# Fourteen units of unmasked rows moved into the triangle's stage, with a joined matmul and a triangle that goes by way of DRAM

## The chip, the cores and the metric

The kernel runs on one core of one Trainium2 chip. The core has a matmul engine (PE, with its weight loads PEld shown apart), a vector engine (DVE), a scalar engine (ACT), a GpSimd engine (POOL) and a sync engine (SP) that only issues transfers. Each engine works through its own list of instructions in order and waits on semaphores. On chip there is SBUF, which engines and transfers use, and PSUM, eight banks of 2 KB in each of 128 partitions, into which PE writes. The metric is the device time in microseconds; the time before is the median of three runs.

## The reference

The input x has the shape (1, 512, 512, 64), in float32. Two layers are applied, each after a group norm over the whole image:

```python
x = x + L0(_gn(x))
x = x + L1(_gn(x))

# L0, with m the 0/1 mask over the 512 positions, D = H = 64
xn = _ln(x, norm_w, norm_b)
left = (xn @ left_w + left_b) * mask          # mask[i, j] = m[i] * m[j]
right = (xn @ right_w + right_b) * mask
left = left * sigmoid(xn @ lgate_w + lgate_b)
right = right * sigmoid(xn @ rgate_w + rgate_b)
out_gate = sigmoid(xn @ ogate_w + ogate_b)
out = einsum('bkjd,bkid->bijd', left, right)   # the "triangle"
out = _ln(out, onorm_w, onorm_b) @ out_w + out_b
return out * out_gate

# L1: the lowest 12 x 12 modes of a 2-D Fourier transform, mixed over
# the channels by complex weights, and transformed back
```

Where a row or a column of the image is masked, the triangle is zero there, so that the output before the gate is a constant row, the transformed bias. The gate is still computed everywhere.

## The kernel before

The kernel sorts the 512 positions by the mask at run time. If at most K = 256 of them are unmasked, which is the case with these inputs, `compact` runs (line 621). Sorted rows 0 to 255 form "half 0", which holds all masked-in rows; rows 256 to 511 form "half 1", which holds only rows whose triangle is zero (these are the change's "unmasked rows", in the sense that no mask or triangle is applied to them).

`compact` has these stages, one after the other:

- **Statistics and compaction** (lines 653 to 700): all of x is read, and the 256 x 256 positions that matter are kept.
- **Projection** (703 to 809): left and right are computed and stored channel by channel to `left_d` and `right_d` in DRAM.
- **Triangle** (848 to 879): for each of 64 channels, left and right are loaded (line 855), each turned by four PE transposes into a PSUM tile (859), copied to SBUF by DVE (864) or ACT (867, two halves), and multiplied in four matmuls (873). DVE applies the masks and writes the result into `tri`, which is the large SBUF array `places`, at a stride of 128 elements (877). No other work runs in this stage.
- **Products and gates** (886 to 1258): one loop over steps `s`, written out by hand, in which each engine's order is the order of the code. Eight steps make a unit. A step handles 8 groups of 64 channels for each of 128 partitions. The first 8 units (`first`) are **products**: the triangle's layer norm and `out_w`, of which the result goes to `u_d` in DRAM. Then follow 32 **gate units** `(jc, half)`, alternating half 1 and half 0 for each of 16 blocks of 32 columns `jc`.
- **Tail** (1260 to 1400): the modes of the second layer, and its output.

In the loop PE works ahead: at step `s` it transposes the data of step `s + LEAD` (`LEAD` = 13, `transpose`, 986), and multiplies by the centring matrix for `s + LEAD - 1` (`centered`, 1005); then it multiplies by the gate's matrix for `s` itself (`times` with `gate_x`, 1002). For products, `centered` instead forms eight matmuls over 64 rows each with `both`, a matrix that holds the centring and `out_w` side by side (1013), and ACT takes the two parts out of PSUM in two instructions (1030, 1031). For gates, ACT takes the transposed data (997) and squares the centred ones (1027). DVE sums the squares over channels (1035), makes the row statistics of the new x (1120), scales by the inverse deviation (1218) and adds the gate's bias (1224). ACT applies the sigmoid (1169). POOL multiplies by the triangle's output, or by the constant row for half 1 (`gated`, 1061), and adds x (`added`, 1065). In products POOL adds a bias (1222).

On the queues: POOL gathers x, 1 MB at a time (637). SP stores the new x (1081), loads the triangle's output of one block by `load_u` (1049), whose 32 transfers each have an address held in a register, loaded first (645), and stores the partial modes of a block (`save`, 1098, four transfers per block); `fetch` and `columns` turn these into sums of modes every 8 units. `load_u` for the next block is issued at each half-1 unit (1242), so once in two units, into one of two buffers, places 5 and 6. x has five buffers (`RING`).

PSUM before: in the products two tiles of two banks each for `y_ps`; in the gates two banks each for `c_ps` and `w_ps`; in both two banks for transposes, one for `scratch` (sums, factors, biases) and one for the modes.

Of the kernel before, what the change touches and what calls it, by code (L numbers as in the profile page):

```python
# [17 lines left out]
P = 128  # L18
N = 512
# [27 lines left out]
def conv_preact_kernel(ctx: ExitStack, tc: tile.TileContext, t: dict):  # L47
# [573 lines left out]
    def compact(fc):  # L621
# [4 lines left out]
        modes_d = dram.tile([N, M2, C], F32, name="modes_d")  # L626
# [203 lines left out]
        with tc.tile_pool(name="tri", bufs=1) as trp:  # L830

            places = trp.tile([P, K * 2 * C], F32, name="places")
            tri = places.rearrange("p (j r c) -> p j r c", r=2, c=C)
# [14 lines left out]
            with tc.tile_pool(name="ti", bufs=4) as ip, tc.tile_pool(name="tt", bufs=3) as tp, tc.tile_pool(  # L848
                name="tpt", bufs=4, space=PSUM
            ) as ps_t, tc.tile_pool(name="tpo", bufs=3, space=PSUM) as ps_o:  # L850
                for c in range(C):
                    sides = []
                    for name, src in (("left", left_d), ("right", right_d)):
                        raw = ip.tile([P, 2, K], F32, name=name + "_raw")
                        nc.sync.dma_start(raw, src[c].rearrange("(b p) k -> p b k", p=P))
                        tps = ps_t.tile([P, 2, K], F32, name="side_ps")
                        for kb in range(2):
                            for b in range(2):
                                nc.tensor.transpose(
                                    tps[:, kb, b * P : (b + 1) * P], raw[:, b, kb * P : (kb + 1) * P], ident  # L860
                                )
                        side = tp.tile([P, 2, K], F32, name=name + "_t")
                        if name == "left":
                            nc.vector.tensor_copy(side, tps)
                        else:
                            for kb in range(2):
                                nc.scalar.mul(side[:, kb, :], tps[:, kb, :], mask_k2[:, kb : kb + 1])
                        sides.append(side)
                    lt, rt = sides
                    ps = ps_o.tile([P, 2, K], F32, name="tri_c_ps")  # L870
                    for r in range(2):
                        for kb in range(2):
                            nc.tensor.matmul(
                                ps[:, r, :], rt[:, kb, r * P : (r + 1) * P], lt[:, kb, :], start=(kb == 0), stop=(kb == 1)
                            )
                    for r in range(2):
                        nc.vector.scalar_tensor_tensor(  # L877
                            tri[:, :, r, c], ps[:, r, :], slot_t[:, r, 1:2], mask_s, ALU.mult, ALU.mult
                        )

# [3 lines left out]
            first = K * 2 // 64  # L884

            units = [(jc, half) for jc in range(NJ) for half in ((1, 0) if jc < NJ - 1 else (0, 1))]
            total_g = (first + len(units)) * SIZE
            with tc.manual_schedule(), tc.tile_pool(name="late", bufs=1) as lp:
# [23 lines left out]
                def columns(h, pool):  # L912

                    q = P if h < 3 else P - JC
                    by = modes_t.rearrange("p (m k) c -> p m (k c)", k=2)
                    ps = pool.tile([P, 4, P], F32, name="t_ps").rearrange("p i k -> p (i k)")[:, : MODES * M2]
                    ps = ps.rearrange("p (m n) -> p m n", m=MODES)
                    for m in range(MODES):
                        nc.tensor.matmul(ps[:, m, :], by[:q, m, :], col_basis[:q, h, :], start=h < 3 or m == 0, stop=h < 3)
                    if h < 3:  # L920
                        nc.vector.tensor_add(sums, sums, ps)
                    return ps

                def fetch(h):

                    q = P if h < 3 else P - JC
                    (nc.scalar if h == 3 else nc.sync).dma_start(modes_t[:q], modes_d[h * P : h * P + q])
# [26 lines left out]
                with tc.tile_pool(name="np_x", bufs=LEAD + 2) as tp, tc.tile_pool(  # L954
# [7 lines left out]
                    ps_y = products.enter_context(tc.tile_pool(name="np_b", bufs=2, space=PSUM))  # L962
# [3 lines left out]
                    for h in range(2):  # L966
                        hs = slice(h * C, (h + 1) * C)
                        nc.vector.tensor_copy(both[hs, :C], center[hs, hs])
                        nc.vector.tensor_copy(both[hs, C:], weights["out"][hs, hs])
# [12 lines left out]

                    def x_of(k):
                        return place(order[k % RING])

                    def transpose(s):
                        k, n = divmod(s, SIZE)
                        flat = (place(k) if k < first else x_of(k - first)).rearrange("p n c -> p (n c)")
# [5 lines left out]
                        if k < first:  # L994
                            nc.scalar.copy(xts[s], tps)
                        else:
                            nc.scalar.activation(xts[s], tps, AF.Identity, bias=ab1[:, 2:3])  # L997
# [7 lines left out]
                    def centered(s):  # L1005
                        if s >= first * SIZE:
                            return times(ps_c, "c_ps", s, center_x)

                        ps = ps_y.tile([P, 2, 4, P], F32, name="y_ps")
                        for i in range(4):  # L1010
                            for h in range(2):
                                hs = slice(h * C, (h + 1) * C)
                                nc.tensor.matmul(ps[:, h, i, :], xts[s][hs, i, :], both[hs], start=True, stop=True)  # L1013

                        xts[s] = tp.tile([P, 4, P], F32, name="xt_c")
                        return ps

                    def raw(s):
                        return xts[s].rearrange("p i (h c) -> p (i h) c", h=2)

                    def squared(s, cps):
# [4 lines left out]
                        if s >= first * SIZE:  # L1026
                            nc.scalar.activation(sq, cps, AF.Square)  # L1027
                        else:
# [14 lines left out]
                    def load(k, r):  # L1043
                        jc, half = units[k]
# [41 lines left out]
                    def transform(k, r):  # L1086
                        jc, half = units[k]
                        if k % 2 == 0 and r == 0:
                            fs[jc] = ps_f.tile([P, N], F32, name="f_ps")
                        for g in range(4):  # L1090
                            o = r * JC + 8 * g
                            nc.tensor.matmul(
                                fs[jc][32 * g : 32 * g + 32, :], hb[:, 2 * half + r, :],
                                x_of(k)[:, o : o + 8, :].rearrange("p j c -> p (j c)"),
                                start=(k % 2 == 0 and r == 0), stop=(k % 2 == 1 and r == 1), tile_position=(0, 32 * g),
                            )

                    def save(jc):
                        ft = places[:, 7 * 64 * C + M2 * C : 7 * 64 * C + 32 * C].rearrange("p (j c) -> p j c", c=C)
                        nc.scalar.copy(ft.rearrange("p j c -> p (j c)"), fs.pop(jc))  # L1100
# [10 lines left out]
                        for g in range(4):  # L1111
                            o = jc * JC + 8 * g
                            queue = nc.scalar if jc == NJ - 2 else nc.sync
                            queue.dma_start(modes_d[o : o + 8].rearrange("j m c -> m j c"), ft[32 * g : 32 * g + M2])

                    def statistics(k, groups):
                        if k % 4 == 0 and 0 in groups:
                            st[k // 4] = s1.tile([P, G, 4, 6], F32, name="stats2c", bufs=2)
                        for g in groups:
                            nc.vector.bn_stats(st[k // 4][:, g, k % 4, :], x_of(k)[:, :, 2 * g : 2 * g + 2])  # L1120
# [22 lines left out]

                    for s in range(-LEAD, total_g + 2 * SIZE):
                        k, n = divmod(s, SIZE)
                        v = k - first

                        def held(i):
                            return 0 <= v - i < len(units)

                        if s + LEAD < total_g:
                            transpose(s + LEAD)
                        wps = cps = None
                        if s + LEAD - 1 == first * SIZE:
# [3 lines left out]
                        if 0 <= s < total_g:  # L1158
                            wps = raw(s) if k < first else times(ps_w, "w_ps", s, gate_x)
                            del xts[s]  # L1160
                        if 0 <= s + LEAD - 1 < total_g:
                            cps = centered(s + LEAD - 1)
                        if n in (0, 4) and held(1):
                            transform(v - 1, n // 4)

                        if n % 2 == 0:
                            i, c = (0, n // 2 - 1) if n >= 2 else (1, 3)
                            if held(i):
                                nc.scalar.activation(zs[v - i, c], zs[v - i, c], AF.Sigmoid)  # L1169
                        if n == 5 and 0 <= k + 1 < first + len(units):  # L1170
# [3 lines left out]
                        if n == 5 and held(1) and v % 2 == 0:  # L1174
                            save(units[v - 1][0])
                        if n == 3 and held(2) and v % 4 == 1:
                            join_squares(v // 4 - 1)

                        if n % 2 == 1:
                            i, c = (0, (n - 3) // 2) if n >= 3 else (1, 3)  # L1180
                            if held(i) and (v - i, c) != (last, 3):
                                gated(v - i, c)
                            elif held(i):
                                finished()
                        else:
                            i, c = (0, (n - 4) // 2) if n >= 4 else (1, 2 + n // 2)
                            if held(i) and (v - i, c) != (last, 3):
                                added(v - i, c)
                        if 0 <= v + 3 < len(units):
                            if n == 3:  # L1190
                                load(v + 3, 0)
                            if n == 6:
                                load(v + 3, 1)
# [284 lines left out]
```

## Time and profile before

| what | value |
|---|---|
| median of 3 runs | 1802.41 us (1800.54 to 1804.09) |
| profiled execution: span, first to last instruction | 1803.7 us |
| PE, DVE, ACT, POOL busy | 90%, 79%, 53%, 52% of the span |
| triangle's stage | about 450 to 648 us |
| products (first to last of their matmuls `y_ps`) | 649.4 to 757 us |
| gates (first `w_ps` to the last bias add) | 775.7 to 1475 us |
| tail | 1475 to 1803.7 us |
| moved by DMA | 484.94 MB, mean 269 GB/s |

The profiled execution is known by its span, and it lies inside the range of the three timed runs, 1.3 us over their median; the page lists nothing outside the span. In a row of the groups of instructions the number after the count is the busy time, then the mean of one instruction in ns, then the engine's idle time just before, and what ended it.

### The profile page before, as it was taken

To read this page: it belongs to the slowest core of one execution; us is meant where nothing else is said; L and a number is where in the kernel's file an instruction comes from. 1 tells how busy PE (TensorE), PEld (TensorE's weight loads), DVE (VectorE), ACT (ScalarE), POOL (GpSimd) and SP (SyncE) were. 2 spreads that over 40 slices of the span, in tenths; PEclk is the share of its full clock that TensorE was granted. 3 is DMA by queue.
4 is the path that set the end of the run, shared out by engine and by line. 5 is a ranking of instruction groups with operands and counts; after the bars stand their busy time and mean duration, and the time that the engine had idled before them with its cause. 6 is when DMAs were issued, how large, how long until landed. Compare 5 with 4: busy or idle time off the path is not lost. (4 is left out here: it accounts for less than half of the span.)

```text
span 1803.7 us, 33076 instructions
## 1 busy us (share of the span) xinstructions
PE 1618.5 (90%) x11174; PEld 1259.6 (70%) x11174; DVE 1426.0 (79%) x2980; ACT 964.2 (53%) x1724; POOL 935.2 (52%) x695
## 2 busy tenths in 40 slices
PE   6879799997899999999999999999999976998772
PEld 6666666662787778887888888888888854665331
DVE  7889678887455547888999999999999995865452
ACT  3655566663222269976777777777777741011000
POOL 4656111111000006788999999999999892111110
PEclk9989899999899999999999999999999977555555
DMA  7999278878655504577777777687677699999999
GB/s 283 389 374 372 98 197 231 228 234 232 206 180 176 178 21 164 222 235 255 259 243 257 264 259 237 227 302 260 236 235 270 215 284 414 426 427 426 427 427 385
DMA packets 194642, 484.94 MB, mean 269 GB/s; under 512 B 35616, under 2 KB 135200, under 8 KB 153504
## 3 DMA queue, kind: packets, MB, share of 16 engines
q1 hardware_dynamic: 158160, 262.09, 41.7%
q0 software_dynamic: 32832, 218.45, 33.4%
q10 hardware_dynamic: 3472, 2.20, 0.5%
q8 instruction: 91, 1.49, 0.3%
q14 instruction: 87, 0.71, 0.1%
HBM read 294.83 MB, written 187.83 MB: 268 GB/s over the span
## 5 line engine op out<-in xcount | busy, mean ns | idle before, releaser
L1002 PE MATMUL w_ps<-gate_x,xt_c 128*128 128x128 f32 x2048 | 280.4, 281 | 29.2 <-DVE z_t L1218 23.8
L1065 POOL TENSOR_TENSOR places<-places,z_t 128x1024 f32<-128x1024 f32 x127 | 301.1, 2371 | 8.1
L1002 PEld LDWEIGHTS w_ps<-gate_x,xt_c 128*128 128x128 f32 x2048 | 252.2, 194 | 44.5 <-DVE z_t L1218 39.9
L1002 PE MATMUL c_ps<-center_x,xt_c 128*128 128x128 f32 x2048 | 276.8, 279 | 0.9 <-ACT xt_c L1031 0.6
L1002 PEld LDWEIGHTS c_ps<-center_x,xt_c 128*128 128x128 f32 x2048 | 252.8, 194 | 3.9 <-ACT xt_c L997 2.2
L1384 PE MATMUL l_ps<-places,rinv 24*128 24x512 f32 x512 | 206.3, 1108 | 29.4 <-DVE places L1391 19.3
L1120 DVE BATCH_NORM_STATS2 stats2c<-places 128x6 f32<-128x128 f32 x1024 | 220.5, 278 | 7.8 <-POOL places L1065 7.8
L1035 DVE TENSOR_REDUCE scratch<-sq_c 128x16 f32<-128x1024 f32 x160 | 194.5, 1216 | 27.9 <-ACT sq_c L1030 23.7
L1169 ACT ACTIVATE z_t<-z_t 128x1024 f32<-128x1024 f32 x128 | 135.5, 1058 | 129.0 <-DVE z_t L1224 113.7
L1222 POOL TENSOR_TENSOR z_t<-z_t,bias_row_out 128x1024 f32<-128x1024 f32 x32 | 75.7, 2365 | 246.5 <-PE y_ps L1013 222.5
L992 PE MATMUL t_ps<-c_ident,places 128*128 128x128 f32 x1280 | 199.5, 279 | 2.0 <-DVE places L877 1.3
L1384 PEld LDWEIGHTS l_ps<-places,rinv 24*128 24x128 f32 x512 | 119.0, 298 | 111.6 <-DVE places L1391 59.4
L992 PEld LDWEIGHTS t_ps<-c_ident,places 128*128 128x128 f32 x1280 | 144.9, 142 | 62.3 <-issue 53.7
L997 ACT ACTIVATE xt_c<-t_ps,ab_xc 128x512 f32<-128x512 f32 x256 | 176.2, 688 | 13.9 <-PE t_ps L992 12.9
L1218 DVE TENSOR_TENSOR z_t<-w_ps,rs_n 128x512 f32<-128x512 f32 x256 | 171.7, 671 | 7.8 <-PE w_ps L1002 7.8
L1027 ACT ACTIVATE sq_c<-c_ps 128x512 f32<-128x512 f32 x256 | 150.7, 589 | 31.6 <-PE c_ps L1002 31.2
L687 DVE BATCH_NORM_STATS2 stats1c<-x_ps 128x6 f32<-128x512 f32 x256 | 156.3, 681 | 13.8 <-PE x_ps L686 12.6
L1224 DVE TENSOR_TENSOR z_t<-z_t,scratch 128x1024 f32<-128x1024 f32 x128 | 156.3, 1221 | 10.3 <-ACT rs_n L1041 4.1
L1061 POOL TENSOR_TENSOR z_t<-z_t,places 128x1024 f32<-128x1024 f32 x64 | 151.8, 2371 | 13.9 <-ACT z_t L1169 13.8
L1391 DVE TENSOR_TENSOR places<-places,l_ps 128x512 f32<-128x512 f32 x176 | 110.4, 683 | 53.7 <-DMA places<-x_h,dst_i 44.4
L1061 POOL TENSOR_TENSOR z_t<-z_t,bias_row_out 128x1024 f32<-128x1024 f32 x63 | 149.3, 2370 | 5.6 <-ACT z_t L1169 4.4
L672 ACT COPY xc<-xg 128x128 f32 x352 | 105.0, 298 | 69.0 <-POOL xc L672 45.2
(213 smaller groups left out, 2619.0 us busy)
## 6 DMA issues: line engine op xcount, KB each, us to landing
x_h<-places SPq DMA_DIRECT2D x64, 1024.0 KB
out_x<-places SPq DMA_DIRECT2D x44, 1024.0 KB
places<-u_d SPq DMA_DIRECT2D x512, 64.0 KB
out_x<-lx_t SPq DMA_DIRECT2D x20, 1024.0 KB
rbc<-rs_d POOLq DMA_DIRECT2D x32, 512.0 KB
left_d<-o_c SPq DMA_DIRECT2D x64, 256.0 KB
right_d<-o_c SPq DMA_DIRECT2D x64, 256.0 KB
left_raw<-left_d SPq DMA_DIRECT2D x64, 256.0 KB
```

The costliest lines, as they stand in the source:

```text
L687: nc.vector.bn_stats(stats[:, 0, 16 * (jc % quarter) + 4 * r + c, :], ps.rearrange("p i k -> p (i k)"))
L992: nc.tensor.transpose(tps[:, i, :], flat[:, o : o + P], ident)
L997: nc.scalar.activation(xts[s], tps, AF.Identity, bias=ab1[:, 2:3])
L1002: nc.tensor.matmul(ps[:, 2 * i : 2 * i + 2, :], xts[s][:, i, :], w, start=True, stop=True)
L1027: nc.scalar.activation(sq, cps, AF.Square)
L1035: nc.vector.tensor_reduce(totals[k % 2][:, 8 * (n - 1) : 8 * (n + 1)], sqs.pop(s // 2), AX.X, ALU.add)
L1061: nc.gpsimd.tensor_mul(zs[k, c], zs[k, c], u)
L1065: nc.gpsimd.tensor_add(xr, xr, zs.pop((k, c)))
L1120: nc.vector.bn_stats(st[k // 4][:, g, k % 4, :], x_of(k)[:, :, 2 * g : 2 * g + 2])
L1218: nc.vector.tensor_mul(z[:, 8 * odd : 8 * odd + 8, :], wps, rs)
L1224: nc.vector.tensor_add(z, z, bias_ps["ogate"].unsqueeze(1).to_broadcast([P, 16, C]))
L1384: nc.tensor.matmul(ps.rearrange("p j o -> p (j o)"), rinv[h, b, :], it[h], start=True, stop=True, tile_position=(32 * g, 0),)
```

## The change

Fourteen of the 16 half-1 gate units, which need nothing of the triangle, are put ahead of the products, and the triangle's instructions are spread over their steps. The order of units becomes 14 early gate units, 8 product units (`None`), gate unit (14, 1), then (jc, 0) for jc = 0 to 15, then (15, 1): 40 units, as before.

- **Centre and gate as one matmul** for the early units: `both` first holds `center_x` and `gate_x`, so that `centered` makes both results in the form that the products used, and ACT copies the second part out of PSUM. `both` is refilled for the products.
- **The triangle** is issued in halves of a channel: `triangle(h)`, `turn_side`, `keep_side`, `masked`. `halves` gives two halves to each of the 12 steps -12 to -1, and spreads the other 104 over the steps 0 to 93. Loads run four sides ahead. The two matmul halves share one PSUM tile `tri_pair` (one bank), and `side_ps` and `y_ps` have one buffer each in that stretch, `y_ps` of two banks.
- **By way of DRAM**: `masked` writes to `staged`, and SP stores each channel to `tri_d`. The products load `tri_d` channel-major, two transfers of 256 KB for each two steps (`load_product`), in place of transposes. Their matmuls then take it directly.
- **`load_u`** is now needed for 16 units in a row and is issued once a unit, at its step 2.
- **Modes** are kept apart by half: `save` runs for each unit but one, and `fetch` and `columns` run eight times in place of four.

```diff
-        modes_d = dram.tile([N, M2, C], F32, name="modes_d")
+        modes_d = [dram.tile([N, M2, C], F32, name=f"modes_d{h}") for h in range(2)]
+        tri_d = dram.tile([C, K, K], F32, name="tri_d")
...
-                for c in range(C):
-                    sides = []
...
-            first = K * 2 // 64
-            units = [(jc, half) for jc in range(NJ) for half in ((1, 0) if jc < NJ - 1 else (0, 1))]
+            early = NJ - 2
+            first = early + K * 2 // 64
+            units = [(jc, 1) for jc in range(early)] + [None] * (first - early) + [(early, 1)]
+            units += [(jc, 0) for jc in range(NJ)] + [(NJ - 1, 1)]
...
+                    ps_y = products.enter_context(tc.tile_pool(name="np_a", bufs=1, space=PSUM))
+                    ps_s = products.enter_context(tc.tile_pool(name="np_i", bufs=1, space=PSUM))
+                    ps_o = products.enter_context(tc.tile_pool(name="np_o", bufs=1, space=PSUM))
+                    tri_pair = ps_o.tile([P, 2, K], F32, name="tri_c_ps")
...
+                    beside(center_x, gate_x)
...
+                    def load_product(q):
+                        for h in range(2):
+                            nc.sync.dma_start(
+                                products_t[q % 4][h * C : (h + 1) * C],
+                                tri_d.rearrange("c j i -> c (j i)")[:, (2 * q + h) * 2 * N : (2 * q + h + 1) * 2 * N],
+                            )
...
+                        if units[s // SIZE] is None:
+                            q, e = divmod(s - early * SIZE, 2)
+                            of = products_t[q % 4][:, e * N : (e + 1) * N].rearrange("p (i k) -> p i k", i=4)
+                        else:
+                            of = xts[s]
                         for i in range(4):
                             for h in range(2):
                                 hs = slice(h * C, (h + 1) * C)
-                                nc.tensor.matmul(ps[:, h, i, :], xts[s][hs, i, :], both[hs], start=True, stop=True)
+                                nc.tensor.matmul(ps[:, h, i, :], of[hs, i, :], both[hs], start=True, stop=True)
...
+                    def load_side(g):
+                        c, right = divmod(g, 2)
+                        nc.sync.dma_start(loose[g % 4], (left_d, right_d)[right][c].rearrange("(b p) k -> p b k", p=P))
+                    def turn_side(g):
+                        tps = side_of[g] = ps_s.tile([P, 2, K], F32, name="side_ps")
...
+                    def keep_side(g):
+                        tps, side = side_of.pop(g), turned_sides[g % 4]
+                        if g % 2:
+                            for kb in range(2):
+                                nc.scalar.mul(side[:, kb, :], tps[:, kb, :], mask_k2[:, kb : kb + 1])
+                        else:
+                            nc.vector.tensor_copy(side[:, 0], tps[:, 0])
+                            nc.scalar.copy(side[:, 1], tps[:, 1])
+                    def triangle(h):
+                        c, b = divmod(h, 2)
+                        lt, rt = (turned_sides[(2 * c + i) % 4] for i in range(2))
+                        tri_of[h] = tri_pair[:, b]
+                        for kb in range(2):
+                            nc.tensor.matmul(
+                                tri_of[h], lt[:, kb, b * P : (b + 1) * P], rt[:, kb, :], start=(kb == 0), stop=(kb == 1)
+                            )
+                    def masked(h):
+                        c, b = divmod(h, 2)
+                        nc.vector.scalar_tensor_tensor(
+                            staged[c % 4][:, b], tri_of.pop(h), slot_t[:, b, 1:2], mask_s, ALU.mult, ALU.mult
+                        )
+                        if b == 1:
+                            nc.sync.dma_start(tri_d[c].rearrange("(b p) i -> p b i", p=P), staged[c % 4])
...
+                    begin, even, until = 1 - LEAD, 0, early * SIZE - LEAD - 5
+                    for h in range(2 * C):
+                        at = begin + h // 2
+                        if at >= even:
+                            done = 2 * (even - begin)
+                            at = even + (h - done) * (until - even) // (2 * C - done)
+                        halves.setdefault(at, []).append(h)
...
                         if s + LEAD < total_g:
                             transpose(s + LEAD)
+                        for h in unmasked:
+                            masked(h)
...
                         if 0 <= s + LEAD - 1 < total_g:
                             cps = centered(s + LEAD - 1)
...
+                        for h in mine:
+                            triangle(h)
+                            turn_next(h + 2)
+                            if h != mine[-1]:
+                                keep_next(h + 2)
...
                         if cps is not None:
                             squared(s + LEAD - 1, cps)
+                        if mine:
+                            keep_next(mine[-1] + 2)
...
+                        for h in mine[:-1]:
+                            masked(h)
+                        unmasked = mine[-1:]
...
-                        if s == first * SIZE:
+                        if s == first * SIZE + 2:
                             load_u(0)
-                        if n == 4 and v % 2 == 0 and 0 <= v < len(units) - 2:
-                            load_u(v // 2 + 1)
+                        if n == 2 and first < k < last - 1:
+                            load_u(k - first)
```

`turn_next` calls `turn_side` and issues the load of the side four further on; `keep_next` calls `keep_side`. In the loop the order within a step is: transposes, the last step's `masked`, `centered`, the modes' matmuls, triangle and turn, ACT's sigmoid, root and `squared`, `keep_next`, then POOL's and DVE's gate work as before.

## The prediction

> **What bounds the kernel now.** First the busy time by stretch: the triangle, the products, the gates (DMA share and GB/s end each line).
>
> ```profile
> core 0: us, PE busy (x) PEld busy (x) DVE busy (x) ACT busy (x) POOL busy (x), PEclk, DMA share, GB/s
> ...
> 450.00:648.00 198.00, 185.44 (x1026) 152.57 (x1025) 108.46 (x201) 53.73 (x128) 0.86 (x2) 0.97 0.57 174
> ...
> 671.00:757.00 86.00, 86.00 (x1032) 71.24 (x1028) 69.37 (x84) 81.00 (x161) 61.35 (x28) 1.00 0.44 170
> ...
> 776.00:1475.00 699.00, 666.41 (x5551) 586.60 (x5549) 670.42 (x1558) 511.04 (x762) 656.37 (x316) 0.98 0.74 250
> ```
>
> In the triangle PE is busy 94% and DVE 55%; in the gates DVE is busy 96%, PE 95%, POOL 94%, ACT 73%. A gate step takes 699/256 = 2.73 us, a unit 21.8. A product step is 109 us/65 steps (648 to 757) = 1.68 us and ACT's (94%). The stages look complementary: that is what could be won. Then the groups that make up DVE's share:
>
> ```profile
> L1120 DVE BATCH_NORM_STATS2 stats2c<-places 128x6 f32<-128x128 f32 x1024 | 220.5, 278 | 7.8 <-POOL places L1065 7.8
> L1035 DVE TENSOR_REDUCE scratch<-sq_c 128x16 f32<-128x1024 f32 x160 | 194.5, 1216 | 27.9 <-ACT sq_c L1030 23.7
> L1218 DVE TENSOR_TENSOR z_t<-w_ps,rs_n 128x512 f32<-128x512 f32 x256 | 171.7, 671 | 7.8 <-PE w_ps L1002 7.8
> L1224 DVE TENSOR_TENSOR z_t<-z_t,scratch 128x1024 f32<-128x1024 f32 x128 | 156.3, 1221 | 10.3 <-ACT rs_n L1041 4.1
> ```
>
> Per pair of gate steps DVE does 8 statistics (1.72 busy), two scalings (1.34), one sum (1.22), one bias (1.22): 5.5, which is the pair's 5.46. Last, the order of time within one channel of the triangle, one group of product matmuls, and SP's queue in the gates:
>
> ```profile
> 550.24 1.59 PEld L873 LDWEIGHTS tri_c_ps<-left_t,right_t 128*128 128x128 f32 x8 [0.32 <-ACT right_t L867]
> 550.24 1.99 PE L873 MATMUL tri_c_ps<-left_t,right_t 128*128 128x256 f32 x8
> 552.27 1.15 DVE L877 SCALAR_TENSOR_TENSOR places<-tri_c_ps,slot_t,mask_s 128x256 f32<-128x256 f32 x2 [1.28 <-PE tri_c_ps L873]
> ...
> 690.58 0.97 PEld L1013 LDWEIGHTS y_ps<-both,xt_y 64*128 64x128 f32 x16 [0.17 <-issue]
> ...
> 1141.37 20.52 SPq L1052 DMA_DIRECT2D places<-u_d  x32
> 1162.15 2.02 SPq L1114 DMA_DIRECT2D modes_d<-places  x4
> ```
>
> A half channel costs PE 0.80 us (4 of the 8), a turned side 0.45 (four transposes), the joined matmul 0.97. DVE's masking, in two halves, starts only after all eight matmuls.
>
> **Early stage: work per engine.** 94 steps carry 104 halves. DVE: 5.46 per pair, plus two maskings and one left copy. Masking into contiguous SBUF is not in the trace: between 0.34 (half of the 128x512 copy at 675 ns) and 0.65 (L877, strided); I take 0.48, nearer the copy. The left half copy is 0.36. Sum 6.8 per pair, 3.4 per step. ACT: 511/256 = 2.0, plus the second copy out of PSUM 0.58, plus per channel two right halves 0.84 and half a left one 0.4, so 0.7 per step: 3.3. PE about 3.1. POOL unchanged, 2.6. With nothing waiting that would be 3.4 us per step.
>
> **The added waits.** Four loops tie the engines: `y_ps`, `side_ps` and `tri_pair` have one buffer each, and the left copy stands in DVE's order ahead of the statistics. While DVE waits there, the statistics, sum, scaling and bias queue behind it, and ACT's sigmoid waits for the bias. Two cases, 42 steps each by the formula of `halves`:
>
> (A) The left copy falls on an even step. DVE masks the last half, PE may then run the next one (0.80), then turn (0.45 and 0.15 until the last has drained), with two wakes: DVE waits 1.5 per pair. 6.8 + 1.5, less 0.3 for instructions that overlap: 8.0 per pair, **4.0 per step**.
>
> (B) It falls on an odd step. Then everything is in one ring: bias ends, sigmoid 1.06, square 0.60, copy 0.58 (these free `y_ps`), matmuls 0.97, half 0.80, turn 0.60, left copy 0.36, statistics 0.86, sum 1.21, scaling 0.68, bias 1.22: 8.9, with wakes and less the overlaps 8.7; ACT's table load (1.28) and DVE's reciprocal (0.54), once in four pairs, add 0.45. **4.55 per step**.
>
> Ten steps hold two halves; keep and turn there precede ACT's squares: 4.3 + 0.8 + 0.6 + 0.5 = 6.2. Two `columns` add 3.4 each (L919: 13.6 us for four). Sum: 42 x 4.0 + 42 x 4.55 + 62 + 7 = **428 us**. Ends: 3.4 x 94 = 320, and 480 if side loads come late too. They share SP with x's stores, which wait for POOL up to 11.9 us now (212.3 us over 30 waits); a side is ordered four halves ahead, 3.6 steps or 15 us, so these waits are covered; without the cover each unit would lose some 7 us.
>
> Here a rule bears. The Trainium skill (PSUM — Partial Sum Buffer, section on bank collisions) says to guard PSUM by bank, not by address, between any two engines. The trace agrees as far as it can: DVE started 39 ns after the eighth matmul though its half was done after the fourth (0.90 us earlier), and the bias (L1224) waited 4.1 us for ACT's root, which shares only the bank `scratch`. So the two halves of `tri_pair` are not two buffers. Guarded by address, case A would be 3.5 and the sum 21 us less.
>
> **Around it.** Lead-in: until the first gather has landed and two sides are turned, 10 us; then 12 steps with two halves, each matmuls 0.97 + half 0.80 + turn 0.60 + left kept 0.5 + squares 1.18, 4.1 us: 49. From 450: 509. Steps 94 to 111 carry no triangle: 18 x 2.73 = 49. Products, steps 112 to 163: no transposes, two ACT instructions for three; POOL's 2.37 per pair and DVE's 0.66 + 0.61 now bind at 1.27 per step, 66; with unit 13's leftovers on POOL and DVE (10), and 31 MB moved (loads of `tri_d`, `u_d`, gathers) at the tail's 415 GB/s = 76, I take 85 (75 to 105). The loads are issued six steps ahead, behind `u_d` stores that wait for POOL; without that cover a landing of some 4 us would show per pair. Mixed steps 164 to 175 as before, (775.7 - 757.5)/12 = 1.52: 18. So the late gates start at 509 + 428 + 49 + 85 + 18 = 1089. In the kernel before, these parts (198 + 128 of products and lead-in + 14 x 21.8 for the same gates) end at 1081. The overlap wins nothing.
>
> **Late stage: SP.** `load_u` moves from once in two units to once a unit. In the trace one takes 3.7 us of register loads and 18.4 to 20.5 us of 32 issues (0.517 apart, at times stalled), even the second, issued with no other in between, 22.4 in all. Each unit now also stores modes (1.7 to 2.0) and x (2 x 0.4), a fetch in four units 0.35 and some 3 us of waiting: 25.3 against DVE's 21.8. Gathers are POOL's and not in this queue. The first load ends 33 us after the gates begin, as before (775.7 to 808.2); it has no slack, since the second gate group that reads it is at step 13 of the stage, 35 us. Over 15 units 15 x 3.4 = 51: 144 x 2.73 + 50 = **443**, range 405 (issues at 0.517, no waits) to 470. Behind a late load wait POOL's gating, then SP's stores and saves.
>
> A second rule: the Trainium skill (DMA: Bandwidth & Descriptors, "Issuing engines are not separate DMA queues") calls the time to initiate transfers "usually small relative to the DMA itself". By bytes a late unit moves 6.3 MB, 15 us at 415 GB/s, so no stretch, and the sum would be 50 less. The row decides: issuing takes 20 us for 2 MB.
>
> **Sum.** 1089 + 443 + tail unchanged 329 = 1861, against the profiled 1803.7: +57; from the median, 1802.4 + 57 = **1860**.
>
> **Rivals.**
> 1. *The loops don't form* (faster): DVE and ACT run ahead of each other as they do over the gates now, and the early steps cost their own work, 3.4: 320 + 7 in place of 428, and 1860 - 101 = 1759. For it: three engines at 94% and more got along in the gates. Against: double buffers there, single here. It decides below 3.9 us per step, where 57 us are recovered. 0.18, with the case that SP is hidden too (1710).
> 2. *The u loads stay hidden*: 1860 - 50 = 1810. For it: they have buffers for two. Against: throughput, not latency, is short. 0.17.
> 3. *DMA saturates*: sides and `tri_d` move in 1 KB pieces (0.57 share at 174 GB/s), u in 512 B pieces. The early stage needs 113 us of all engines for sides, half as much for `tri_d` and 13 for each of 14 units: 352 of 478; late, 16.1 (0.74 of 21.8) and half a u load more, 1 MB at the sides' 305 GB/s or 3.4: 19.5 of 25. If landings delay both, 4.9 per step and 27 per unit: 1860 + 40 + 25 = 1925. 0.15.
> The sum as worked out has 0.50.
>
> **Range.** 1770 to 1915: it leaves out the outer parts of rivals 1 and 3; the likeliest alone is 1820 to 1895 (early stage ±30, products ±12, late ±15). A measurement here tells 0.2% (3.6 us) from no change. Faster 0.19, same 0.03, slower 0.78.
>
> **What would show it.** The stretch from 510 to 940 should show 4.3 to 4.6 us per early gate step, DVE idle ahead of the left copy (waiting for `side_ps`) and PE for `tri_c_ps`, with DVE about 80%. Late, SP's loads should follow each other with no gap, POOL waiting for `u_d`, units of 25 us and DVE at 85%. It is wrong if early steps take 3.5, or if late units stay at 21.8.

## The result and the profile after

The changed kernel takes **1973.7 us** (1968.8 to 1978.9), the one before 1801.5 beside it: 1.095 times as long (95% interval 1.093 to 1.098). Slower was right; 1860 was 114 us short, and outside the range. First the busy time by stretch, cut where the z scalings of the gate steps (L1333) show the stages to begin: lead-in, early steps with the triangle, steps 94 to 111, products, mixed steps, late gates, tail.

```profile
core 0: us, PE busy (x) PEld busy (x) DVE busy (x) ACT busy (x) POOL busy (x), PEclk, DMA share, GB/s
450.00:528.00 78.00, 65.47 (x490) 52.13 (x492) 23.94 (x46) 37.92 (x84) 2.18 (x3) 0.90 0.65 218
528.00:976.00 448.00, 356.14 (x2912) 280.96 (x2908) 308.80 (x701) 295.98 (x529) 238.54 (x114) 0.93 0.60 199
976.00:1034.00 58.00, 37.27 (x342) 26.16 (x342) 55.23 (x121) 38.70 (x62) 42.45 (x19) 0.75 0.63 175
1034.00:1122.00 88.00, 69.71 (x821) 59.91 (x818) 74.56 (x123) 54.21 (x108) 66.36 (x30) 0.93 0.98 322
...
1150.00:1643.00 493.00, 402.15 (x3098) 360.44 (x3097) 373.70 (x855) 291.06 (x432) 363.43 (x175) 0.88 0.72 232
```

No engine is full in either long stage. In the early one DVE is at 69% and PE at 79%; in the late one the best, PE, is at 82%, where the kernel before had three engines at 94% and more in its gates. By the first and last scaling of each stage, against the terms of the prediction and against the same work before:

| part | predicted | measured | over |
|---|---|---|---|
| start to first scaled step | 509 | 528.2 | +19 |
| steps 0 to 93, with 104 halves | 428 | 448.9 | +21 |
| steps 94 to 111 | 49 | 57.4 | +8 |
| products, to step 163 | 85 | 96.2 | +11 |
| mixed, to step 175 | 18 | 18.9 | +1 |
| late gates | 443 | 491.5 | +49 |
| tail | 329 | 331.7 | +3 |

That is the whole difference between 1861 and the span of 1972.9. The parts up to the late gates end at 1149.6. Taken by the scalings too, the same work ended at 1084 before (the first of the gates at 779.1, and 14 units of 21.8): +65. The late gates take 491.5 for 389 (1084 to 1473.4): +102. With 1 to 2 in the tail these are the 169 us lost.

The granted clock was 0.93 in the early steps and 0.88 in the late gates, where the gates before had 0.98. It came back to 0.99 and 0.97 in the two runs below that take a wait away and leave PE's work as it is (e3_left_act, e1_u_one). PE's busy time fell with it from 356 to 329 us early and from 402 to 373 late. As an estimate from these figures, the clock can account for no more than 28 of the 82 us that the early stage gains in e3 and 30 of the 100 that the late one gains in e1, and PE was full in neither stage of the changed kernel. No run changed the clock alone.

Next, the waits over the whole run, and one early pair of steps on DVE, PE and ACT in order of time.

```profile
engine line waited for: us in total, times, longest us
...
DVE places L1158 <- PE side_ps L1147: 181.1, 64, 11.0
...
PEld tri_c_ps L1167 <- DVE places L1174: 85.6, 43, 4.1
...
ACT places L1159 <- DVE places L1158: 75.8, 53, 5.3
PE tri_c_ps L1167 <- DVE places L1174: 74.2, 48, 3.9
...
ACT places L1119 <- DMA modes_d<-places: 71.7, 13, 7.2
```

```profile
start us, us, engine line op out<-in xcount [idle before <-releaser]
...
713.24 0.48 DVE L1174 SCALAR_TENSOR_TENSOR places<-tri_c_ps,slot_t,mask_s 128x256 f32<-128x256 f32 x1
...
713.77 1.13 PE L1167 MATMUL tri_c_ps<-places 128*128 128x256 f32 x4 [1.60 <-DVE places L1174]
...
716.33 0.48 DVE L1174 SCALAR_TENSOR_TENSOR places<-tri_c_ps,slot_t,mask_s 128x256 f32<-128x256 f32 x1
...
716.96 1.10 PE L1167 MATMUL tri_c_ps<-places 128*128 128x256 f32 x4
...
717.90 0.60 PE L1147 MATMUL side_ps<-c_ident,places 128*128 128x128 f32 x4
...
718.53 0.42 DVE L1158 COPY places<-side_ps 128x256 f32<-128x256 f32 x1 [1.72 <-PE side_ps L1147]
...
718.88 0.86 DVE L1184 BATCH_NORM_STATS2 stats2c<-places 128x6 f32<-128x128 f32 x4
718.99 0.37 ACT L1159 COPY places<-side_ps 128x256 f32<-128x256 f32 x1 [0.98 <-DVE places L1158]
```

The forecast loops are there: PE waits for the masking of the half before (713.77), DVE then waits 1.72 us at the left copy (718.53) for the side that PE turns after the next half (717.90), and the statistics queue behind it. One link was not forecast: ACT's half of the left copy waits for DVE's (718.99), though both only read `side_ps` and write different parts of `places`. (POOL writes other parts of `places` at the same time, from 717.00 to 719.35, so it isn't that array that is kept to one engine; the two share the tile `side_ps`.) Last, SP's queue in the late gates.

```profile
1273.10 19.89 SPq L1065 DMA_DIRECT2D places<-u_d  x32
1293.10 0.36 SPq L1094 DMA_DIRECT2D x_h<-places  x1
1293.55 3.82 SPq L1133 DMA_DIRECT2D modes_d<-places  x4
1297.48 0.35 SPq L1094 DMA_DIRECT2D x_h<-places  x1
1301.92 18.28 SPq L1065 DMA_DIRECT2D places<-u_d  x32
```

Between these rows no gap is over 0.2 us but the 4.1 us of register loads ahead of the second u load (1297.83 to 1301.92). One turn is 28.8 us here, 29.1 as the mean of 14 (1181.62 to 1589.19), against DVE's 21.8 us of work per unit.

### The profile page after: what moved, and what is told of

The parts are those of the page before. It is cut to its first block, busy times and chain, and to the rows that moved or that the text cites. A ratio compares the mean times of both kernels' runs of the same rounds, so it can differ in the third digit from the quotient of the medians.

```text
span 1972.9 us, 33265 instructions
## 1 busy us (share of the span) xinstructions
PE 1588.0 (80%) x11014; PEld 1217.3 (62%) x11014; DVE 1412.6 (72%) x2988; ACT 1018.8 (52%) x1853; POOL 935.3 (47%) x695
## 5 line engine op out<-in xcount | busy, mean ns | idle before, releaser
L1074 POOL TENSOR_TENSOR z_t<-z_t,bias_row_out 128x1024 f32<-128x1024 f32 x63 | 148.7, 2361 | 296.2 <-ACT z_t L1275 194.4
L1184 DVE BATCH_NORM_STATS2 stats2c<-places 128x6 f32<-128x128 f32 x1024 | 220.5, 279 | 13.4 <-POOL places L1078 13.3
L1046 DVE TENSOR_REDUCE scratch<-sq_c 128x16 f32<-128x1024 f32 x160 | 194.7, 1217 | 47.5 <-ACT sq_c L1035 33.8
L1167 PE MATMUL tri_c_ps<-places 128*128 128x256 f32 x512 | 154.5, 428 | 77.5 <-DVE places L1174 74.2
L999 PE MATMUL c_ps<-center_x,xt_c 128*128 128x128 f32 x1152 | 164.4, 289 | 44.6 <-ACT xt_c L994 43.9
L999 PEld LDWEIGHTS c_ps<-center_x,xt_c 128*128 128x128 f32 x1152 | 150.4, 204 | 47.7 <-ACT xt_c L994 46.8
L992 PE MATMUL t_ps<-c_ident,places 128*128 128x128 f32 x1024 | 170.5, 294 | 6.6 <-DMA places<-in_x,src_i 6.6
L999 PE MATMUL w_ps<-gate_x,xt_c 128*128 128x128 f32 x1152 | 166.7, 292 | 11.1 <-DVE z_t L1333 10.7
L1167 PEld LDWEIGHTS tri_c_ps<-places 128*128 128x128 f32 x512 | 92.6, 201 | 119.4 <-DVE places L1174 85.6
L999 PEld LDWEIGHTS w_ps<-gate_x,xt_c 128*128 128x128 f32 x1152 | 152.7, 207 | 18.7 <-DVE z_t L1333 18.7
L1158 DVE COPY places<-side_ps 128x256 f32<-128x256 f32 x64 | 27.2, 425 | 181.1 <-PE side_ps L1147 181.1
L1015 PE MATMUL y_ps<-both,xt_y 64*128 64x128 f32 x1792 | 136.2, 294 | 19.8 <-ACT xt_c L1042 19.6
L1015 PEld LDWEIGHTS y_ps<-both,xt_y 64*128 64x128 f32 x1792 | 114.4, 196 | 42.2 <-ACT xt_c L1042 28.8
```

What stands on the lines that cost most here:

```text
L992: nc.tensor.transpose(tps[:, i, :], flat[:, o : o + P], ident)
L999: nc.tensor.matmul(ps[:, 2 * i : 2 * i + 2, :], xts[s][:, i, :], w, start=True, stop=True)
L1015: nc.tensor.matmul(ps[:, h, i, :], of[hs, i, :], both[hs], start=True, stop=True)
L1046: nc.vector.tensor_reduce(totals[k % 2][:, 8 * (n - 1) : 8 * (n + 1)], sqs.pop(s // 2), AX.X, ALU.add)
L1074: nc.gpsimd.tensor_mul(zs[k, c], zs[k, c], u)
L1167: nc.tensor.matmul(tri_of[h], lt[:, kb, b * P : (b + 1) * P], rt[:, kb, :], start=(kb == 0), stop=(kb == 1))
```

## The experiments

My theory: two separate causes, the loops through `side_ps` and `tri_c_ps` early (+65), and SP's issue time late (+102). Stage times are by the scalings, as above. Where no other base is named, a kernel is the changed one with one edit.

**The late stage: SP's issues, or something else?** In e1_u_one one load takes the place of 32, in pieces of the same size, though always of the same rows:

```
-for j, slot in enumerate(slots_of(mybir.EngineType.SP, jc)):
-    nc.sync.dma_start(us[jc][:, j], u_d[:, bass.ds(slot, 1)]...)
+nc.sync.dma_start(us[jc], u_d[:, 0 : 2 * JC : 2])
```

> Leaves out that each block's rows of u are chosen: load_u becomes one static transfer of the same 32 pieces of 512 B per partition, without register loads, so the bytes and pieces stay and SP's time per late unit falls from about 29 us to 6. SP-queue theory: late stage (first to last gate group read from w_ps) from 492 us to 385-415, total 1973.7 to 1870-1900. Rival, that the bytes in small pieces set the late pace: 480-495, total unchanged within 15. Rival, that the sums of modes (fetch and columns, a 10 us longer unit in every four) have their own cost: late 420-450.

It took 1872.4 us (1.041 of before, 1.037 to 1.044). The late stage fell from 491.5 to 391.2, the early one stayed (447.8).

```profile
core 0: us, PE busy (x) PEld busy (x) DVE busy (x) ACT busy (x) POOL busy (x), PEclk, DMA share, GB/s
1150.00:1541.00 391.00, 372.70 (x3096) 327.53 (x3094) 368.84 (x848) 286.58 (x428) 361.90 (x174) 0.97 0.94 296
```

DVE is back at 94% and PE at 95%, and as many pieces pass at 296 GB/s instead of 232: bytes were not the limit. Units take 21.0, and 24.9 where modes are fetched, where they took up to 38: the waits for fetches and saves (L1119, 71.7 us in the changed kernel, none in this stage of e1) were SP's lateness too.

Two attempts to relieve SP otherwise. e8_columns_later adds the modes' sums one unit later (`k == ready + 3` for `+ 2`), so that PE need not wait for the fetch behind a u load:

> The sums of modes are formed one unit later, so that PE does not wait for the fetch that stands behind a u load (4 waits, 31 us). If SP's queue sets the late pace, the time lost moves elsewhere: late stage 475-492, total 1957-1976. If these waits are a cost of their own: late 455-465, total 1938-1948.

1978.4 us, no gain. The long units went (26 to 30 all through), and the stage took 481.1, 10 less: most of the wait moved, and SP's turn stayed (28.4 us as the mean of 14). The early stage took 455.7, 7 more, for which no reason was found. e2_saves_act issues the stores of modes from ACT's queue:

```
-queue = nc.scalar if (jc, half) == (NJ - 2, 0) else nc.sync
-queue.dma_start(modes_d[half][o : o + 8]..., ft[...])
+nc.scalar.dma_start(modes_d[half][o : o + 8]..., ft[...])
```

> The four stores of partial modes per unit are issued by ACT in place of SP, in all units. SP-queue theory: SP loses 3.4-4.5 us of 29 per late unit, and ACT no longer waits for stores that stand behind a u load (71.7 us of waits go): late stage 492 to 410-440, total 1900-1930; early stage unchanged within 10. Rival, bytes: unchanged within 15.

A miss: 2074.6 us, 100 slower, with 555.2 late and 468.6 early. In SP's queue of this kernel a wait stands that the changed kernel does not have:

```profile
engine line waited for: us in total, times, longest us
...
SPq L1065 <- DMA modes_d<-places: 101.8, 13, 11.0
```

The trace gives the semaphore that each DMA signals: SP's and ACT's share eight (99 to 106), taken in turn, and each DMA waits for its semaphore's last one. At 1286.4 SP stops within a u load; ACT issues its four stores from 1294.21 on, the first on 104; SP goes on at 1295.89, on 104. So a u load of SP waits until ACT has come to its stores, although the two write different tensors. This is read from the trace; no run gave the stores a queue or semaphores of their own, and the 20 us that the early stage lost were not traced.

**The early stage: which loop?** e3_left_act takes the left copy from DVE:

```
-nc.vector.tensor_copy(side[:, 0], tps[:, 0])
-nc.scalar.copy(side[:, 1], tps[:, 1])
+for kb in range(2):
+    nc.scalar.copy(side[:, kb], tps[:, kb])
```

> The left side's first half is copied by ACT too, so DVE no longer waits for a turned side. Ring theory (DVE's copy ahead of its statistics, with the one-bank tiles): the 181 us that DVE waits before the copy go, early stage (steps 0 to 93) 449 to 350-390, 3.7-4.1 us a step, total 1890-1925, though ACT gets 26 us more. Rival, that ACT and PE set the early pace by their work: 440-475, total 1965-2000.

1889.8 us (1.050, 1.048 to 1.053): early 366.6 for 448.9, 3.9 per step, late 489.2. Its early stage:

```profile
core 0: us, PE busy (x) PEld busy (x) DVE busy (x) ACT busy (x) POOL busy (x), PEclk, DMA share, GB/s
526.00:893.00 367.00, 328.61 (x2908) 261.45 (x2904) 292.48 (x652) 307.20 (x581) 239.19 (x115) 0.99 0.74 243
```

ACT, which got the work, is busy 84%: it was not the limit. The sides and `tri_d` move as before, in less time (243 GB/s for 199), so DMA was not the limit of the early stage either. e7_copy_behind leaves the copy with DVE and moves it behind the statistics in the order of the step; ACT's copies of sides stand in the same place of the code and move with it, behind the copy of a save in one step of eight:

> The left copy moves behind the statistics in DVE's order, nothing else. Ring theory: DVE's wait for a turned side (181 us) shrinks by up to 0.86 us per copy, early stage 449 to 405-430, total 1930-1955. If the place in DVE's order does not matter: within 8 us of 1974.

1928.1 us, early 401.5: the same work in another order is worth 46 us, more than half of e3's gain. It is mainly what queues behind the wait that costs, as predicted. e6_tri_two and e9_tri_apart ask about the other wait, PE's for the masking of the neighbouring half. Both give the gates' transposes one buffer in place of two, to make room; e6 spreads the one tile over two banks, e9 makes two tiles:

```
-tri_pair = ps_o.tile([P, 2, K], F32, name="tri_c_ps")
e6: +tri_pair = ps_o.tile([P, 2, 2 * K], F32, name="tri_c_ps")[:, :, :K]
e9: +tri_pair = [ps_o.tile([P, 2, K], F32, name=f"tri_c_ps{b}")[:, 0] for b in range(2)]
```

> The two halves of tri_pair get a bank each; the bank is taken from the transposes, which keep one. If halves in one bank exclude each other (guard by bank): PE no longer waits for the masking of the half before (160 us of waits in the early stage fall below 80), early stage 449 to 410-435, total 1935-1965. If the guard is by address: early 445-465, total unchanged or longer by the single transpose bank.

> As e6_tri_two (one buffer for the transposes of the gates), but the triangle's two halves are two tiles of their own, each in its own bank, where e6 had one tile over two banks and PE's waits for the masking stayed (L1167 for L1174, 85.7 + 73.7 us). If the wait is for the neighbouring half, by bank or by tile: those two rows go, case A of the prediction falls to 3.5 per step, the early stage from 446 to 420-430, the time to 1945-1960. If the ring through the left copy is what sets the step (bias, sigmoid, square, copy, matmuls, half, turn, left copy), the rows go and their time comes back as DVE's wait for side_ps or PE's for the y_ps of ACT: early 438-450, 1964-1978.

e6: 1974.0 us, early 445.9, no gain. From the waits of its early stage:

```profile
PEld tri_c_ps L1167 <- DVE places L1174: 85.7, 43, 4.1
...
PE tri_c_ps L1167 <- DVE places L1174: 73.7, 46, 3.9
```

Within half a microsecond they are the changed kernel's (85.6 and 74.2 in the same stretch), though the halves lie in separate banks. e9: 1933.3 us (1.073, 1.069 to 1.077), early 408.6, better than expected. The same part of its list:

```profile
POOL z_t L1074 <- ACT z_t L1275: 222.5, 41, 81.7
DVE places L1158 <- PE side_ps L1147: 91.2, 45, 4.3
PEld y_ps L1015 <- ACT xt_c L1042: 73.4, 55, 2.9
PE y_ps L1015 <- ACT xt_c L1042: 60.6, 49, 2.7
```

PE's wait for L1174 is gone, DVE's for `side_ps` falls from 129.8 (early, changed kernel) to 91.2, and the next link shows, `y_ps`, which has one buffer. The two kernels have the same banks, and e9 is 37 us shorter early than e6. So the wait goes with the tile: the program guards this one as a whole, and banks of their own don't free its halves. Whether two tiles within one bank would be free of each other was not tried. e12_apart_left joins e9 and e3:

> The edits of e9_tri_apart and e3_left_act together. Alone they took 40 us (early 448.9 to 408.6) and 82 us (to 366.6). If they are two links of one chain (PE waits for the masking because DVE stands at the left copy), most of the smaller gain is already in the larger: with the copy on ACT, PE waited for L1174 only 20 us in the early stage, so early 350-364, time 1872-1888. If they are separate delays, the gains add: early 327, time 1850. The late stage, SP's, stays at 486-491.

1895.5 us (1.050, 1.046 to 1.053), early 367.4: nothing beyond e3. The masking and the left copy are two links of one chain. Its early stage:

```profile
core 0: us, PE busy (x) PEld busy (x) DVE busy (x) ACT busy (x) POOL busy (x), PEclk, DMA share, GB/s
526.00:893.00 367.00, 334.38 (x2929) 266.96 (x2928) 290.03 (x644) 305.44 (x583) 238.24 (x114) 0.98 0.74 245
```

PE is now busy 91%, 3.56 us per step: at its present speed little is left to gain for this mix of work.

**What the overlap is worth.** e4_no_tri leaves the 104 halves of the early stage out:

> Leaves out the triangle's 104 halves of steps 0 to 93 (loads, turns, products, masking, stores to tri_d); the products then read left_d. What the early gates cost alone in the joined form: by DVE's work 2.75 a step, 258 us for 94 steps, total about 1785; if the single y_ps already limits them, 300-340, total 1830-1865. The difference from 449 is what the 104 halves cost; the triangle alone took 3.0 us a channel, 156 us for 52.

1812.0 us, early 281.0:

```profile
core 0: us, PE busy (x) PEld busy (x) DVE busy (x) ACT busy (x) POOL busy (x), PEclk, DMA share, GB/s
528.00:809.00 281.00, 206.14 (x2104) 151.74 (x2104) 249.88 (x550) 240.97 (x381) 239.21 (x115) 0.91 0.54 179
```

So the halves cost 448.9 - 281.0 = 168 us within the gates. In a stage of their own they had cost 104 x 198/128 = 161. The overlap won nothing; with e3's edit they cost 366.6 - 281.0 = 86. The early gates alone take 2.99 us per step, where a gate step took 2.73 before and I expected 2.75: the joined form with one `y_ps` has a price of its own, some 24 us over 94 steps, which no run took apart.

**Do the two causes make up the whole?** e10_both_causes has the edits of e1 and e3:

> Both halves of left copied by ACT, and one static load of u in place of 32 by register (its output leaves out the choice of u's rows, as e1 did). If the two causes are independent, in two stages that follow each other, the gains add: 1973.7 - 83.9 - 101.3 = 1788.5, early 365-368, late 390-394. If one hides part of the other (SP's queue is shared by the sides' loads and by u's, and DMA by all), 1800-1850.

1788.7 us, against 1788.5 from the sum of the gains; early 366.6, late 392.6. The gains add up, so the two causes are independent, and together (185 us) they are more than the 172 that the change lost. It is 0.993 of before (0.991 to 0.995), 13 us less; smaller losses, in the lead-in, the steps 94 to 111 and the products, are still in it. It is no version to use, since u's rows are not chosen in it.

**One part alone.** e11_tri_dram is the kernel before, with only the way through DRAM:

```
+staged = tp.tile([P, 2, K], F32, name="staged")
 for r in range(2):
     nc.vector.scalar_tensor_tensor(
-        tri[:, :, r, c], ps[:, r, :], slot_t[:, r, 1:2], mask_s, ALU.mult, ALU.mult
+        staged[:, r], ps[:, r, :], slot_t[:, r, 1:2], mask_s, ALU.mult, ALU.mult
     )
+nc.sync.dma_start(tri_d[c].rearrange("(b p) i -> p b i", p=P), staged)
...
+load_product((s + LEAD + 5) // 2)
```

> The kernel before with one part of the change alone: the triangle's output goes to DRAM channel-major, masked into a contiguous tile, and the products load it so, without transposes; order, gates and u loads as before. Products: ACT has two instructions for three, a step 1.54 (12.3 per unit, measured after) for 1.68, so 65 x 0.14 = 9 us less; the last stores and the first loads are exposed between the stages: 8 to 12 us more; the triangle stays PE's (198 us) if DMA's share only rises from 0.57 to some 0.85. Sum 1795-1812, about as before. If DMA then bounds the triangle (the share reaches 0.95 and more), 1820-1850.

1804.4 us, 1.0016 of before (1.0007 to 1.0026): no difference of weight. From the end of the preparation to the gates:

```profile
core 0: us, PE busy (x) PEld busy (x) DVE busy (x) ACT busy (x) POOL busy (x), PEclk, DMA share, GB/s
450.00:660.00 210.00, 196.93 (x1166) 163.74 (x1164) 99.15 (x203) 61.89 (x144) 0.00 (x0) 0.96 0.84 253
660.00:780.00 120.00, 95.23 (x1092) 84.79 (x1089) 93.14 (x112) 79.46 (x153) 81.31 (x38) 0.94 0.90 297
```

DMA is busy 84 and 90% where it was 57 and 43% before, yet the first scaling of the gates comes at 776.3 us, where it came at 779.1. PE waits 6.75 us once, for the first loads, and a products unit takes 12.5 us for 13.4. The last one takes 23.0 for 13.8: PE waits there for loads of `tri_d` that come late (6.1 us between 740 and 766). On the whole the detour is neither the loss nor a gain.

**A version faster than before?** e5_order10 takes e3's and e8's edits and fewer early units; five second-half units return among the late ones, to give SP room:

```
-early = NJ - 2
+early = 10
-units += [(jc, 0) for jc in range(NJ)] + [(NJ - 1, 1)]
+for jc in range(NJ):
+    if jc in (0, 3, 6, 9, 12):
+        units.append((others.pop(0), 1))
+    units.append((jc, 0))
```

> Ten early units in place of 14; the other half-1 units stand among the half-0 units, one ahead of each three, so that a u load is due in three units of four; the left copy is ACT's (as in the run with that edit alone) and sums of modes are formed one unit later. If both causes are right they share out: early stage (62 steps, 1.68 halves a step) 62 x (2.99 + 1.68 x 0.82) = 271, late stage (22 units) at DVE's 21.8 with SP just covered, 480-495, total 1785 (1770-1805), below the kernel before. If SP's queue or the rings still bind: late 530+, total 1830+.

A miss: 1897.2 us (1.050, 1.048 to 1.052). In this order two fetches of mode rows come one unit apart, and the second overwrites the first before its sums are taken; the amount of work is unchanged. Against e3, 32 early steps less saved only 366.6 - 326.8 = 40 us, since 104 halves now share 62 steps and the single buffers set 3.1 us per half. The late stage grew from 489.2 to 529.8, the same 41: eleven u loads still follow another with no unit between, and its 175 steps take 52 more than 2.73 each. What is moved out of one limit meets the other. No version that does the whole computation beat the kernel before.

## Why the prediction was wrong

**Right.** The direction, and the mechanism in both stages: the loops form, the overlap wins nothing (168 us for 161), SP binds late, the tail stays. Rival 1 (the loops don't form) falls: only e3's edit brings a step to the 3.9 us from which it decides. Rival 2 (u stays hidden) falls with the solid queue. Rival 3 (DMA saturates) came closest in total and was wrong in cause: e3 moves the same sides and e1 as many pieces of u, each in less time. Of the two rules weighed, the row was the right choice for issue time, and not enough so: the Trainium skill (DMA: Bandwidth & Descriptors, on issuing engines) would have had the late stage 50 us below 443, and it measured 49 above. Its rule on banks (PSUM — Partial Sum Buffer) left me with the right wait for a reason that the runs don't bear out: e6 shows that the wait stays with the halves in two banks. It isn't contradicted, since two tiles in one bank were not tried. The rows that I read as agreeing with it could not tell: in both cases the two engines shared the tile as well as the bank.

**The terms that failed.**
1. *Late stage, 25.3 per u load* (+49, the largest). I summed 22.4 for a u load, 1.7 to 2.0 for four stores of modes and 0.8 for x. A turn in the queue above has 24.0 (19.89 and 4.1 of register loads), 3.8 and 0.7; the mean of 14 turns has 23.9, 3.7 and 0.9. The excess is 14 x (29.1 - 25.3) = 53, about half of it in the stores. In the trace before they stood directly behind the u load and took 1.7 in most cases, and up to 4.0 (at 860.6); now an x store of 1 MB stands between, and they take 2.9 to 4.5. Why the new place costs more is open. e1 confirms that SP's turn is what binds: 101 us go with it.
2. *Case A, 4.0 per step* (part of +21). Pairs of steps with the left copy on an even step took 9.4 us as the mean, where I had 8.0, and those on an odd one 9.3 for 9.1. That is 29 us over 21 pairs of case A; the other terms together were 8 too long. DVE's wait ahead of the left copy was 2.7 us in A (20 copies), where I had 1.5. I had put the statistics, sum and bias into B's ring alone, but the large sum (L1046, 1.21) falls on even steps, not on odd. The mode transform on PE (1.07) and ACT's table loads, which I charged to B only, can fall into A's ring too; how much each adds, no run shows. The price of PE's wait for the neighbouring half was 40 us (e9) where I had 21.
3. *Lead-in* (+19). From the first squares (469.0) to those of step 0 (526.5) the twelve steps took 57.5 us for 49, most of them 4.66 for 4.1. In the step from 470.19 to 474.85 the joined matmuls took 1.09, the half 0.75, the turn 0.85, the left copy 0.79 and the squares with the second copy 1.18: the turn and the left copy (0.60 and 0.5 in the prediction) were too small, the latter because ACT's half starts when DVE's ends, which I had as parallel. The first squares also came 6 us later than my terms give (463), and step 0 runs for some 5 us before its first scaling, which 509 left out.
4. *Products 85 and steps 94 to 111* (+19). The products' units of 12.0 to 13.4 hold what I took (1.5 to 1.7 per step). The first took 19.2, with the leftovers that I had put at 10, and the last 22.0: PE waits there for loads of `tri_d` (5.8 us between 1096 and 1120), the landings that I took to be covered. e11 has the same long unit at the end of its products, so it comes with the way through DRAM. The last early steps ran at 3.2, not 2.73; e4, without the halves, shows 2.99 for the joined form, and the rest is open (the granted clock was 0.75 there). Every kernel with this order of units has these losses (54.9 to 61.5 for steps 94 to 111, 96.2 to 99.8 for the products).

Early stage and products ended inside the ranges that I gave them. The late stage did not (491.5 for 405 to 470), the lead-in and the steps 94 to 111 had no range, and the errors all had one sign: so the sum left its range of 1770 to 1915.

## What to carry to other kernels

When work is moved so that a queue or a single-buffered tile becomes the pace, take its cycle from a solid stretch in the order that it will have, with the gaps between groups in it. The sum of its instructions' durations in another order was 3.8 us too low here, in 29.1. Before overlapping two stages, draw the ring through each tile with one buffer: here the same 104 halves cost 168 us inside the gates, 161 alone, and 86 when one 0.4 us copy left the queue of the engine that everything else waits for. Where two stages are each paced by something other than an engine, moving work from one to the other trades one for the other (e5: 40 us for 41).

## What the runs showed of the hardware

- In these programs the DMAs of SP's and ACT's queues are tied to each other: they take eight semaphores in turn over both, so u loads on SP waited 101.8 us in 13 places for stores that ACT issued late (e2).
- A tile in PSUM that DVE and ACT both only read was read in turn (75.8 us in 53 waits of L1159 for L1158), and PE's wait for a neighbouring half stayed with one tile over two banks and went with two tiles (e6, e9). Both are waits that the program sets; what the chip would allow without them no run shows.
- 32 loads of 64 KB with an address from a register cost SP 24 us per 2 MB in its solid queue; one load of as many pieces cost it 0.4, and the traffic then rose from 232 to 296 GB/s.
